# Four graph layers on one core: order of the degree, packing and normalizing steps, wider rows of pairs, and earlier loads of layer 3's mask bytes

## The chip, the cores and the metric

The kernel runs on one core of a Trainium2 chip. The metric is the device time of one launch in microseconds (us), the median of three runs. One further execution was taken with the hardware profiler; all views below are of that execution.

## What is computed

Input is x (2708 x 512, float32) and a symmetric 0/1 adjacency adj (2708 x 2708, under 1% ones). Four layers follow each other, each as `x = layernorm(x + layer(x))`:

```python
deg = max((adj != 0).sum(-1), 1)
L0: relu((dinv * (adj + I) * dinv @ x + x) @ W0 + b0)        # dinv = rsqrt(deg)
L1: (dis[:, None] * adj * dis[None, :] @ x) @ W1.T + b1      # dis = (adj.sum(1) + 1e-8) ** -0.5
L2: twice:                                                   # two attention layers
    Wh, Ws = split(x @ W2[l]); a = softmax(Wh @ Ws.T) * adj
    x = leaky_relu(a @ Wh + x, 0.01)
L3: adj @ (x @ W3) + b3                                      # 8 heads of 64 columns, as one 512-column product
```

## The kernel before, in words

**Tiles.** The 2708 nodes are 22 blocks of 128 rows; the last has 20 (block 21, "the 20-row block"). Output columns are taken in six chunks `CH` (512, 512, 512, 512, 384, 276 nodes; the last holds blocks 19, 20 and 21), input rows in six `GROUPS` (4, 4, 4, 4, 3, 3 blocks). SBUF has a pool of 82 general pages (`page`), which are used in turn, so that a new page waits for the last use of an old one; 11 wider ones (`wide`) take what the gathers fetch. PSUM has two halves of four banks (`bank`).

**Order.** Every instruction goes through `Ordered.issue` (L70 in every view), which makes each engine run its instructions in the order in which the program writes them. So the order of work is that of the Python code, engine by engine, DMA queues included: most loads and writes are issued by SP, gathers, x's writes and the residual loads (`xres`) by POOL. A blocked instruction holds all that stand behind it on its engine.

**Layers 0 and 1, and the rest of layer 3** are a list `run.seq` of steps (layer, chunk k, group g). `step` (L1066) first calls `before_products`, which loads the bytes of the adjacency (`at`) for two steps ahead (`load`) and prepares one step ahead (`prepare`, L788): ACT casts bytes to products' operands m and, in chunk 0, halves of x (`xh` on ACT, `xl` on DVE, a split of float32 in two). Then `multiply` issues PE's products into `acc`; `ends` does, a step or two later, what belongs to the chunk before: `project` (products mm with the weights), `combine` and `finish` (residual, statistics, normalizing, write). At the last group `evict` copies acc to ht. In layer 0, `examine` (L820) has DVE count and check each mask by pairs of blocks (`odd`, `part`); `degrees` (L891) adds the parts into `both` at the fifth group, and at the sixth multiplies them by ones on PE (`deg`, `cnt`), evicts these to `dg` and `cnt`, multiplies xt by dg on POOL and takes the roots (`dis`, `rdeg`). The product of the next step's acc takes the bank that deg had. The masks are written to memory as bytes and read back by all later layers. In layer 1, `prepare` also reduces the bytes by quarters of a block into `feeds` on DVE, inside the preparing.

**Packing.** After a chunk of layer 1, `index` (L1123) makes lists of the rows that each block needs, as a generator of DVE and PE stretches: products `rank` and `rest`, DVE steps keep to `up` between them, then `place`, a check of overflow (`top`, `bad`), and `one_hot` and the product `list`. `beat` (L586) runs one stretch of it at two of every three calls; `ends` and the attention's score loop call it.

**Attention.** Layers 2a and 2b run in `layer` (L1730) with a model clock (`advance`, `later`, `until`): scores sp, their greatest, shift, exponentials and sums (`soften`, L1539) on DVE and ACT; s and z (`project_steps`, L1408) are written to `pairs` in memory, a row per giver node. `fetch` (L1596) gathers 128 of these rows with one indirect DMA issued by POOL, of s and z side by side, 2,176 to 2,560 bytes of a row; `weigh` multiplies them on PE into acc. `end` and `normalize` (L1707) finish a block and write it. `pairs` is [2, rows, 768], s 128 | z 512 | s 128, so a row has a pitch of 3,072 bytes, and each z is written twice. DVE copies z out of PSUM.

**Layer 3's beginning.** During layer 2b, `early` (L599) puts the products of layer 3's first two chunks and first four groups between the attention's steps (`fill`); the sums go to pages `begun` by ACT's copies. `layer` asks for its first pieces after scores 5, 11 and 19 of the last chunk: nothing, then two loads of bytes, then `prepare` of the first four blocks (their xh and xl). Further bytes are loaded two steps ahead.

**The end.** After the last step, the run ends by `project`, `combine` and `finish` of the last chunk, block by block: 19, 20, then the 20-row block, which was computed as four partial products and is summed by a copy and three adds (`total`) and one more add.

Of the kernel before, what the change touches and what calls it, by code (L numbers as in the profile page):

```python
# [39 lines left out]
PAD = 16  # L40
FAR = 4096
# [473 lines left out]
class Fast:  # L515
# [17 lines left out]
    def run(self):  # L533
        kernel, nc = self.k, self.nc
        with ExitStack() as ctx:
# [34 lines left out]
            for i, n, ps in self.project(ly, k):  # L570
                self.finish(ly, k, [(i, n, self.combine(ly, k, 0, i, n, ps))])
# [27 lines left out]
    def early(self, run):  # L599
# [8 lines left out]
        for t in range(4 * TWO):  # L608
            ly, k, g = seq[t]
            if t < 2:  # L610
                self.attention.need(GROUPS[t + 2][1] - 1)
            self.load(*seq[t + 2])
            if t == 4:
                self.load_weights(ly)
            if t == 4 * TWO - 1:
                self.attention.need(GROUPS[4][1] - 1)
                for j in range(*GROUPS[4]):
                    ly.rows[j] = self.attention.made[j]
            self.prepare(*seq[t + 1])
            if g == 3:  # L620
                ly.begun[k] = []
            for n, j in enumerate(range(*GROUPS[g])):
                if t == 0:
                    self.multiply(ly, k, g, [j])
                else:
                    self.multiply(ly, k, g, ds=[n])
                if g == 3:
                    b = self.page(f"begun{k}_{n}")
                    self.nc.scalar.copy(b[:, : CH[k][1]], ly.acc[k][n][:, : CH[k][1]])
                    ly.begun[k].append(b)  # L630
                self.attention.advance(2 * cost(CH[k][1]))
                yield True
# [15 lines left out]
    def normalize(self, mv, rows):  # L648

# [3 lines left out]
        self.rsqrt(y, mv[:, :m, 1], LN_EPS)  # L653
# [21 lines left out]
    def rsqrt(self, dst, src, eps):  # L675
# [7 lines left out]
        nc.scalar.activation(t, v, AF.Sqrt)  # L683
        nc.vector.reciprocal(y, t)
# [63 lines left out]
    def load(self, ly, k, g):  # L748
# [6 lines left out]
        if ly.number == 0:  # L755
            tiles = []
            for j in js:
# [11 lines left out]
                for d in range(DC):  # L769
                    self.nc.sync.dma_start(at[d * QW : (d + 1) * QW, :cw], few)  # L770
        else:
            at = self.page(f"at{ly.number}_{k}_{g}", U8, (P, DC, BANK))
            self.nc.sync.dma_start(
                at[:, : len(js), :cw], self.k.masks[k][:, js[0] : js[-1] + 1, :]
            )
            tiles = [at[:, q, :] for q in range(len(js))]
            ly.done["bytes", k, g] = at
        ly.done["at", k, g] = tiles
# [9 lines left out]
    def prepare(self, ly, k, g):  # L788
# [7 lines left out]
        for j, at in zip(range(*GROUPS[g]), ats):  # L796
# [4 lines left out]
            ms.append(m)  # L801
        ly.done["m", k, g] = ms
        if ly.number == 0:
            self.examine(ly, k, g, ats)
        if ly.number == 1:
            at, (j0, j1) = ly.done.pop(("bytes", k, g)), GROUPS[g]
            feeds = self.k.feeds.rearrange("p i q j -> p j (i q)")
            i0, full = c0 // QW, cw // QW
            sets = [(j0, j1, P)] if j1 < NB else [(j0, j1 - 1, P), (j1 - 1, j1, QW)]
            for q0, q1, n in ((0, full, QW), (full, -(-cw // QW), cw % QW)):  # L810
                for a, b, rows in sets if q0 < q1 else ():
                    v = at[:rows, a - j0 : b - j0, q0 * QW : q0 * QW + (q1 - q0) * n]
                    nc.vector.tensor_reduce(
                        feeds[:rows, a:b, i0 + q0 : i0 + q1],
                        v.rearrange("p j (q i) -> p j q i", i=n),
                        AX.X,
                        ALU.max,
                    )

    def examine(self, ly, k, g, ats):  # L820
        nc, cw = self.nc, CH[k][1]
# [4 lines left out]
        for q in range(0, len(ats), 2):  # L826
# [24 lines left out]
            else:  # L851
                nc.vector.tensor_add(p, p, t)

# [37 lines left out]
    def degrees(self, ly, k, g):  # L891

        nc, cw = self.nc, CH[k][1]
        i0, n = CH[k][0] // P, len(blocks_of(k))
        if g == len(GROUPS) - 2:
            ly.both = both = self.page(f"both{k}", BF)
            if cw % P:
                nc.vector.memset(both, 0.0)
            nc.vector.tensor_add(both[:, :cw], ly.part[k][:, 0, :cw], ly.part[k][:, 1, :cw])
            return  # L900
        both = ly.both
# [3 lines left out]
        for q in range(n):  # L905
# [6 lines left out]
            )  # L912
        dg = self.page(f"dg{k}")
        nc.vector.tensor_scalar(dg[:, :cw], ps[:, :cw], 1.0, 1.0, ALU.max, ALU.add)
        cnt = self.small.tile([P, DC], FP, tag="cnt", name=f"cnt_sb{k}")[:, :n]
        nc.vector.tensor_copy(cnt, pc[:, :n])
        xt = ly.done["xt", k]
        for c in range(DC):
            nc.gpsimd.tensor_mul(xt[c][:, :cw], xt[c][:, :cw], dg[:, :cw])
        self.rsqrt(self.k.dis[:, i0 : i0 + n], cnt, DEG_EPS)  # L920
# [20 lines left out]
    def project(self, ly, k):  # L941
# [3 lines left out]
        for i, lo, n in blocks_of(k):  # L945
# [44 lines left out]
    def sum(self, ly, i, n, ps):  # L990
        nc, x = self.nc, ly.done.pop(("xres", i))
        if n <= QW:
# [15 lines left out]
    def finish(self, ly, k, parts):  # L1008
# [14 lines left out]
        return out  # L1023
# [10 lines left out]
    def before_products(self, run, t):  # L1034
# [23 lines left out]
        if t + 1 < len(seq):  # L1058
            self.prepare(*seq[t + 1])
        if ly.number == 0 and g == len(GROUPS) - 2:  # L1060
            self.degrees(ly, k, g)
# [4 lines left out]
    def step(self, run, t):  # L1066
# [19 lines left out]
        if g == (4 if ly.number == 3 and k < TWO else 3):  # L1086
            self.residual(ly, k)
            if k == len(CH) - 1 and ly is not run.layers[-1]:
                self.load_weights(run.layers[1])
        if g == len(GROUPS) - 1:  # L1090
            if ly.number == 3:
                self.biased(ly, k)
            if ly.number == 0:
                self.degrees(ly, k, g)
# [3 lines left out]
            if k in ly.acc:  # L1098
                self.evict(ly, k)
            run.before, run.phase = (ly, k), 0  # L1100
            if ly.number == 1:
# [3 lines left out]
    def ends(self, run, g):  # L1105

        nc, (ly, k) = self.nc, run.before
        if g == 0:
            run.parts = self.project(ly, k)
            run.x = []  # L1110
        if g in (0, 1):
# [11 lines left out]
    def index(self, k):  # L1123
# [80 lines left out]
        nc.vector.tensor_add(place, place, place_r)  # L1204

        top = tile_("top", [P, n], FP)
        nc.vector.tensor_mul(place_r, rank, rest[:, :, PAD:])
        nc.vector.tensor_reduce(top, place_r, AX.X, ALU.max)
        for q, (i, _, _) in enumerate(blocks_of(k)):
            room = sum(t >= nq * ONLY for ts in lists_of(i) for t in ts) * P  # L1210
            nc.vector.tensor_scalar(
                kernel.bad[:, kernel.nbad + i : kernel.nbad + i + 1],
                top[:, q : q + 1],
                1.0 - room,
                0.0,
                ALU.add,
                ALU.max,
            )
# [8 lines left out]
        for q in range(n):  # L1227
            rows, both = self.one_hot(i0 + q, row[:, q, :], which[:, q, :])
            yield "PE"
# [72 lines left out]
class Attention:  # L1302
# [7 lines left out]
    def __init__(self, fast):  # L1310
# [7 lines left out]

        self.pairs = [
            [  # L1320
                self.scratch.tile([2, NP, D + 2 * P], FP, tag=f"p{a}{b}", name=f"pairs{a}{b}")
# [9 lines left out]
    def blank(self):  # L1331

        blank = [self.page(f"blank{e}") for e in range(2)]
        for e, t in enumerate(blank):
            self.nc.gpsimd.memset(t, 0.0)
            for pairs in (p for ly in self.pairs for p in ly):
                for r in range(2):
                    c = e * D
                    w = min(D, D + 2 * P - c)
                    self.nc.sync.dma_start(pairs[r, N:, c : c + w], t[: NP - N, :w])  # L1340
# [67 lines left out]
    def project_steps(self, ly, k):  # L1408
# [19 lines left out]
        for i, lo, n in blocks_of(k):  # L1428
# [16 lines left out]
            if n > QW:  # L1445
                nc.vector.tensor_copy(z[:n], ps[:n])
            for b in range(2):
                nc.sync.dma_start(
                    ly.pairs[b][:, i * P : i * P + n, P : P + D].rearrange("r j d -> j r d"),
                    z[:n].unsqueeze(1).to_broadcast([n, 2, D]),  # L1450
# [79 lines left out]
    def load_masks(self, ch):  # L1530
        for j0, j1 in GROUPS:
            a = self.page(f"a{ch.name}_{j0}", U8, (P, DC, BANK))
            self.nc.sync.dma_start(
                a[:, : j1 - j0, : ch.cw], self.k.masks[ch.k][:, j0:j1, :]
            )
# [3 lines left out]
    def soften(self, ch):  # L1539
# [23 lines left out]
        for q0, q1, w in self.parts(ch):  # L1563
            for side in range(2):
                qs = [q for q in range(q0, q1) if q % 2 == side]
                if not qs:
                    continue
                r0, m, c = qs[0] // 2, len(qs), side * (P + D)
                e = ch.s[j][:n, qs[0] * P : qs[0] * P + w].unsqueeze(1)
                if m > 1:  # L1570
                    e = ch.s[j][:n, :].rearrange("j (r x) -> j r x", x=2 * P)
                    e = e[:, r0 : r0 + m, side * P : side * P + w]
                nc.sync.dma_start(
                    ch.ly.pairs[ch.k % 2][
                        r0 : r0 + m, j * P : j * P + n, c : c + w
                    ].rearrange("r j i -> j r i"),
                    e,
                )
# [17 lines left out]
    def fetch(self, ch):  # L1596
# [5 lines left out]
        if q not in ch.x:  # L1602
# [7 lines left out]
        h = t // ONLY if t < QUARTERS * ONLY else (0, QUARTERS - 1)[q % 2]  # L1610
        first, width = (P, D + (h + 1) * QW) if q % 2 else (h * QW, D + P - h * QW)
# [3 lines left out]
            in_=ch.ly.pairs[ch.k % 2].rearrange("r j d -> (r j) d"),  # L1615
            in_offset=bass.IndirectOffsetOnAxis(ap=self.k.givers[:, i, t : t + 1], axis=0),
            element_offset=(q // 2) * NP * (D + 2 * P) + first,
# [25 lines left out]
    def weigh(self, wait=False):  # L1643
# [18 lines left out]
        for h, g in enumerate(gs):  # L1662
            lo, m = (0, w) if len(gs) == 1 else (h * QW, QW)
            e, z = (D + lo, 0) if q % 2 else (0, P - lo)
# [42 lines left out]
    def normalize(self, ch):  # L1707
        self.f.normalize(ch.mv, [(r, r, w) for r, w in ch.ends])
        for (i, _, _), (r, _) in zip(ch.blocks, ch.ends):
            self.nc.sync.dma_start(self.k.saved[2][i], r)  # L1710
            self.made[i] = r
# [18 lines left out]
    def layer(self, ly, chunks, fill):  # L1730
        f = self.f
        self.chunks, self.made = chunks, {}
        for k, ch in enumerate(chunks):
# [4 lines left out]
            for n, j in enumerate(js):  # L1738
# [15 lines left out]
                if n in (5, 11, 19) and k + 1 == len(chunks):  # L1754
# [17 lines left out]
        self.shift_rows(last)  # L1772
        self.until(self.clock + 3, fill)
# [112 lines left out]
```

## Time and profile before

| | |
|---|---|
| runs | 2347.88, 2351.14, 2351.31 us (median 2351.14) |
| profiled execution | 2336.56 us, of which the span is 2334.30 |
| busy of PE | 2275.3 us, 97% |
| busy of DVE, ACT, POOL | 1428.0, 663.8, 708.3 us |
| mean granted clock of PE | 0.99 |
| DMA | 463.50 MB, 199 GB/s over the span |

A line of the page's groups gives line, engine, operation, output and inputs, count, then busy time and mean ns of one, then the idle time ahead of them on that engine and what ended it. In a timeline a row gives start, duration, and in brackets the idle time before and its releaser. Busy times of DVE, ACT and POOL lie under PE's wherever PE doesn't wait for them. The page's slices show the kernel's stages: layer 0's groups end at 303 us, layer 1 reduces its bytes into feeds until 606, scores of the attention run from 780 to 1971, the products of what was gathered from 945 to 2117 in two stretches (POOL's two high stretches), and layer 3's last products start at 2318:

```profile
DVE  6777886786655529658667511228769778624523
POOL 3334431111000000635466450001635557452000
```

### The profile page before, as it was taken

The page shows a single profiled execution, that of the slowest core. Times are in us where ns is not written, and L with a number is a line of the kernel's source. Part 1 is how long each engine was busy: PE and PEld are TensorE (multiplying, and loading weights), DVE is VectorE, ACT ScalarE, POOL GpSimd, SP SyncE. Part 2 cuts the span into 40 slices and gives each one's busy share as a digit, 9 for nine tenths or more (in the row PEclk, how much of TensorE's full clock was granted, in tenths as well). Part 3 has the DMA queues.
Part 4 walks back from the last instruction along what each step waited for, and adds up shares of the span by engine and source line. Part 5 has one row for each costly group of instructions (what it writes and reads, how often), then busy time and mean ns, then how long its engine had stood idle before and what let it go on. Part 6 is the DMA issues. An engine that isn't in the chain of part 4 may idle for free. (4 is left out here: it accounts for less than half of the span.)

```text
span 2334.3 us, 26143 instructions
## 1 busy us (share of the span) xinstructions
PE 2275.3 (97%) x8525; PEld 1293.5 (55%) x8525; DVE 1428.0 (61%) x2832; ACT 663.8 (28%) x1334; POOL 708.3 (30%) x823
## 2 busy tenths in 40 slices
PE   9999999999999999999999999999999999899997
PEld 6676767778644444443555444444443455565675
DVE  6777886786655529658667511228769778624523
ACT  7444352222110123223232210113222324431211
POOL 3334431111000000635466450001635557452000
PEclk9999999999999999999999999999999999899999
DMA  9966652222434404869699996305868799883311
GB/s 339 292 179 174 177 176 79 75 81 79 174 132 175 146 0 148 304 211 307 217 342 327 299 381 245 136 5 165 297 220 292 251 308 333 282 270 116 116 50 43
DMA packets 324247, 463.50 MB, mean 199 GB/s; under 512 B 66370, under 2 KB 201962, under 8 KB 324100
## 3 DMA queue, kind: packets, MB, share of 16 engines
q1 hardware_dynamic: 255444, 246.57, 32.1%
q0 software_dynamic: 68656, 215.15, 27.7%
q8 instruction: 69, 1.13, 0.2%
q14 instruction: 78, 0.64, 0.1%
HBM read 307.75 MB, written 153.85 MB: 198 GB/s over the span
## 5 line engine op out<-in xcount | busy, mean ns | idle before, releaser
L70 PE MATMUL sp<-xs,wst_sb 128*128 128x512 f32 (+3 forms) x2112 | 800.2, 545 | 0.0
L70 POOL DMA_INDIRECT g<-pairs,givers x510 | 526.5, 1032 | 881.0 <-issue 372.8
L70 PEld LDWEIGHTS sp<-xs,wst_sb 128*128 128x128 f32 (+1 forms) x2112 | 380.2, 186 | 409.8 <-issue 326.2
L70 PE MATMUL acc<-m,xh 128*128 128x512 f32 (+4 forms) x1584 | 569.8, 381 | 17.8 <-ACT begun L70 8.3
L70 PE MATMUL acc<-m,xl 128*128 128x512 f32 (+4 forms) x1584 | 552.4, 367 | 0.5 <-DVE xl L70 0.5
L70 PEld LDWEIGHTS acc<-m,xh 128*128 128x128 f32 (+1 forms) x1584 | 290.3, 189 | 84.0 <-issue 23.6
L70 PEld LDWEIGHTS acc<-m,xl 128*128 128x128 f32 (+1 forms) x1584 | 290.5, 190 | 45.5 <-issue 5.3
L70 PE MATMUL acc<-g 128*32 128x512 f32 (+1 forms) x1020 | 261.4, 609 | 2.5 <-DMA g<-pairs,givers 2.3
L70 ACT ACTIVATE s<-s 128x512 f32<-128x512 f32 (+3 forms) x264 | 151.5, 579 | 334.6 <-DVE s L70 334.5
L70 ACT COPY s<-sp 128x512 f32<-128x512 f32 (+2 forms) x252 | 132.6, 528 | 400.2 <-PE sp L70 397.2
L70 DVE TENSOR_TENSOR top<-top,s 128x512 f32<-128x512 f32 (+2 forms) x240 | 149.2, 622 | 152.1 <-ACT s L70 149.7
L70 PE MATMUL mm<-w,ht 128*128 128x512 f32 (+1 forms) x528 | 224.2, 596 | 5.0 <-DVE ht L70 5.0
L70 ACT CAST m<-at 128x512 fp32r<-128x512 uint8 (+5 forms) x396 | 199.3, 566 | 75.3 <-DMA at<-mask 38.0
L70 DVE TENSOR_TENSOR s<-s,shift 128x512 f32<-128x512 f32 (+3 forms) x264 | 162.6, 619 | 34.2 <-ACT shift L70 34.2
L70 DVE TENSOR_TENSOR s<-s,a 128x512 f32<-128x512 f32 (+3 forms) x264 | 166.1, 629 | 20.3 <-DMA a<-mask 11.3
L70 DVE TENSOR_TENSOR sum<-sum,s 128x512 f32<-128x512 f32 (+4 forms) x252 | 156.5, 621 | 17.4 <-ACT s L70 17.4
L70 PEld LDWEIGHTS mm<-w,ht 128*128 128x128 f32 (+1 forms) x528 | 96.2, 187 | 122.1 <-issue 111.3
L70 PE MATMUL wst<-xt,mixed 128*128 128x512 f32 (+2 forms) x384 | 151.0, 545 | 1.9 <-ACT mixed L70 1.9
L70 PEld LDWEIGHTS acc<-g 128*32 128x32 f32 (+1 forms) x1020 | 74.6, 135 | 140.5 <-issue 116.6
L70 PE MATMUL z<-w,xt 128*128 128x512 f32 (+1 forms) x352 | 151.0, 596 | 0.0
L70 DVE COPY z_sb<-z 128x512 f32<-128x512 f32 (+1 forms) x44 | 30.3, 690 | 178.3 <-PE z L70 175.1
L70 POOL DMA_DIRECT2D x<-o x44 | 26.0, 597 | 357.0 <-DVE o L70 352.8
(168 smaller groups left out, 1543.6 us busy)
## 6 DMA issues: line engine op xcount, KB each, us to landing
pairs<-s SPq DMA_DIRECT2D x378, 128.0 KB
pairs<-z_sb SPq DMA_DIRECT2D x84, 512.0 KB
at<-in_adj_t SPq DMA_DIRECT2D x84, 256.0 KB
xres<-x POOLq DMA_DIRECT2D x44, 256.0 KB
x<-o POOLq DMA_DIRECT2D x43, 256.0 KB
x<-x SPq DMA_DIRECT2D x37, 256.0 KB
at<-mask SPq DMA_DIRECT2D x32, 256.0 KB
xt<-t SPq DMA_DIRECT2D x32, 256.0 KB
```

The source lines that it names most:

```text
L70: ins = call(*args, **kw)
```

## The change

It touches the order of several stages and the shape of one memory tensor.

1. `examine` of layer 0 becomes a generator that stops after each pair of blocks. For chunks above 0, in group 0, only the first pair is examined at `prepare`; the rest (`checked`) follows the eviction of the chunk before.
2. `degrees` is split: `degree_ends` makes the products, then dg and cnt, then the multiplications and roots. At the last chunk of layer 0 its middle part runs after the first cast of the next step's `prepare`, whose reduction into feeds (`note`) and layer 1's weight loads come after the eviction. `before_products` no longer prepares across the layer boundary.
3. In `index` the check (top, bad) runs behind the first `one_hot`; one more `beat` comes in `ends` at the last chunk of layer 1.
4. z of layer 2a is evicted by ACT, no longer by DVE.
5. `pairs` has one row of 2,048 floats per node, z 512 | s 256 | z 512 | s 256 | z 512; z is written three times, s in pieces of 256 floats; gathers take their parts from these rows. The pages for mask bytes are as wide as the chunk, not 512, so that the pieces of a load join.
6. The normalizing in layer 2b stops after the root's issue on ACT; the rest is put 4 us of the model clock later.
7. `layer` asks for layer 3's halves no longer after score 19 but after `shift_rows`; `early` loads bytes five groups further ahead (`load_bytes`).
8. At the end of layer 3 the 20-row block is projected first, is summed by four adds straight into x, and is normalized together with block 19; block 20 follows.

```diff
             ly, k = run.before
-            for i, n, ps in self.project(ly, k):
-                self.finish(ly, k, [(i, n, self.combine(ly, k, 0, i, n, ps))])
+            parts = self.project(ly, k)
+            for some in (parts[:-1], parts[-1:]):
+                made = []
+                for i, n, ps in some:
+                    made.append((i, n, self.combine(ly, k, len(made), i, n, ps)))
+                self.finish(ly, k, made)
...
             ly, k, g = seq[t]
+            for later in seq[t + 2 if t == 0 else t + 6 : t + 7]:
+                self.load_bytes(*later)
             if t < 2:
                 self.attention.need(GROUPS[t + 2][1] - 1)
...
         nc.scalar.activation(t, v, AF.Sqrt)
+        yield True
         nc.vector.reciprocal(y, t)
...
+    def load_bytes(self, ly, k, g):
+        if ("bytes", k, g) in ly.loaded:
+            return
+        ly.loaded.add(("bytes", k, g))
+        (j0, j1), cw = GROUPS[g], CH[k][1]
+        at = self.page(f"at{ly.number}_{k}_{g}", U8, (P, DC, cw))
+        self.nc.sync.dma_start(at[:, : j1 - j0, :], self.k.masks[k][:, j0:j1, :])
...
         if ly.number == 0:
-            self.examine(ly, k, g, ats)
+            self.examining = self.examine(ly, k, g, ats)
+            if k == 0 or g > 0:
+                self.checked()
+            else:
+                next(self.examining)
...
-        for i, lo, n in blocks_of(k):
+        for i, lo, n in sorted(blocks_of(k), key=lambda b: b[2] > QW):
...
         nc, x = self.nc, ly.done.pop(("xres", i))
+        if n <= QW and ly.number == 3:
+            for c in range(DC):
+                nc.vector.tensor_add(x[:n], x[:n], ps[c * QW : c * QW + n, :])
+            return x
...
-        if t + 1 < len(seq):
+        if t + 1 < len(seq) and seq[t + 1][0].number == ly.number:
             self.prepare(*seq[t + 1])
...
-            if k == len(CH) - 1 and ly is not run.layers[-1]:
-                self.load_weights(run.layers[1])
...
             if ly.number == 0:
-                self.degrees(ly, k, g)
+                ends = self.degree_ends(ly, k)
+                next(ends)
+                if k == len(CH) - 1:
+                    note = self.prepare(
+                        *run.seq[t + 1], between=lambda: next(ends), late=True
+                    )
+                for _ in ends:
+                    pass
...
                 self.evict(ly, k)
+            if ly.number == 0:
+                self.checked()
             run.before, run.phase = (ly, k), 0
+            if ly.number == 0 and k == len(CH) - 1:
+                note()
+                self.load_weights(run.layers[1])
...
+            if ly.number == 1 and k == len(CH) - 1:
+                self.beat()
...
             rows, both = self.one_hot(i0 + q, row[:, q, :], which[:, q, :])
+            if q == 0:
+                examine()
             yield "PE"
...
-                self.scratch.tile([2, NP, D + 2 * P], FP, tag=f"p{a}{b}", name=f"pairs{a}{b}")
+                self.scratch.tile([NP, 2 * PAIR + D], FP, tag=f"p{a}{b}", name=f"pairs{a}{b}")
...
-            if n > QW:
+            if n > QW and a == 0:
+                nc.scalar.copy(z[:n], ps[:n])
+            elif n > QW:
                 nc.vector.tensor_copy(z[:n], ps[:n])
             for b in range(2):
+                rows = ly.pairs[b][i * P : i * P + n, :]
                 nc.sync.dma_start(
-                    ly.pairs[b][:, i * P : i * P + n, P : P + D].rearrange("r j d -> j r d"),
-                    z[:n].unsqueeze(1).to_broadcast([n, 2, D]),
+                    bass.AP(rows.tensor, rows.offset, [rows.ap[0], (PAIR, 3), (1, D)]),
+                    z[:n].unsqueeze(1).to_broadcast([n, 3, D]),
                 )
...
     def normalize(self, ch):
-        self.f.normalize(ch.mv, [(r, r, w) for r, w in ch.ends])
-        for (i, _, _), (r, _) in zip(ch.blocks, ch.ends):
-            self.nc.sync.dma_start(self.k.saved[2][i], r)
-            self.made[i] = r
+        work = self.f.normalizing(ch.mv, [(r, r, w) for r, w in ch.ends])
+        next(work)
+        def rest():
+            for _ in work:
+                pass
+            for (i, _, _), (r, _) in zip(ch.blocks, ch.ends):
+                self.nc.sync.dma_start(self.k.saved[2][i], r)
+                self.made[i] = r
+        self.later(4, rest)
...
-                if n in (5, 11, 19) and k + 1 == len(chunks):
+                if k + 1 == len(chunks) and n in ((5, 11, 19) if ly.number == 0 else (5, 11)):
                     next(fill)
...
         self.shift_rows(last)
+        if ly.number == 1:
+            next(fill)
         self.until(self.clock + 3, fill)
```

## The prediction

> **What bounds the kernel now.** I read the page's busy times, then PE's waits, then the timelines of the engines at each of those waits, and the chain for the end.
>
> ```profile
> PE 2275.3 (97%) x8525; PEld 1293.5 (55%) x8525; DVE 1428.0 (61%) x2832; ACT 663.8 (28%) x1334; POOL 708.3 (30%) x823
> ```
>
> PE is the bound: 97% of the 2334.3 us span. No product is removed, so only PE's idle time, its slow time and the end can go. The waits of PE ("waited for: us in total, times, longest us"):
>
> ```profile
> PE acc L70 <- ACT begun L70: 8.3, 1, 8.3
> PE acc L70 <- DVE dg L70: 6.3, 2, 5.3
> PE mm L70 <- DVE ht L70: 5.0, 3, 2.3
> PE list L70 <- DVE both L70: 4.2, 3, 2.7
> PE rest L70 <- DVE up L70: 3.5, 1, 3.5
> PE tr_mx L70 <- DVE wide L70: 3.5, 1, 3.5
> PE acc L70 <- ACT m L70: 3.2, 1, 3.2
> PE tr_top L70 <- DVE top L70: 2.7, 1, 2.7
> PE acc L70 <- DMA g<-pairs,givers: 2.3, 5, 0.6
> ```
>
> With the smaller ones about 42 us in all, nearly every line a single event. Some are paid twice. Two stretches of the windows (start and end, length, busy time of PE, PEld, DVE, ACT and POOL, granted clock, DMA share, GB/s):
>
> ```profile
> 658.00:668.00 10.00, 6.46 (x17) 2.65 (x17) 9.00 (x31) 1.17 (x2) 1.51 (x3) 1.00 0.15 57
> 2026.30:2036.50 10.20, 5.70 (x13) 4.46 (x14) 5.21 (x14) 7.28 (x16) 1.00 (x1) 0.50 0.75 202
> ```
>
> After the 8.30 us gap the clock is 0.50 for 10.2 us, and a product takes 0.80 us rather than 0.39. Such stretches follow the gaps at 66.8, 303.7, 408.5, 782.8, 1981.4, 2022.1 and 2130.9 (3.4, 6.8, 3.4, 3.4, 3.4, 10.2 and 3.4 us): 34 us at half rate, 17 lost. The 3.54 us gap at 658.7 and the 2.67 us one at 1912.3 brought none. With the 19.5 us tail (2314.8 to 2334.3), some 78 us are to be had at most; each part below gets its share.
>
> **The change part by part** (gain in us, then both ends).
>
> *First examine deferred.* Ahead of dg (62.48) DVE runs odd, odd and an add of part, 0.69 each; they go behind evict: 2.06 us earlier dg and ht, against gaps of 0.98 (dg) and 2.25 (ht), and 1.7 of half clock. In the later chunks DVE stood idle before dg, so nothing changes there. 3.0 (2.0 to 3.7).
>
> *Degrees at the layer boundary.* PE's 5.35 us wait at 303.7 is the product that needs the bank which dg empties. On DVE (start, duration, what it is):
>
> ```profile
> 306.79 2.29 DVE L70 TENSOR_REDUCE feeds<-at 128x64 bf16<-128x2048 uint8 x1
> 308.98 0.43 DVE L70 TENSOR_SCALAR dg<-deg 128x276 f32<-128x276 f32 x1
> ```
>
> dg (0.43) moves ahead of the later xl's, which waited 4.67 and 0.90 us, and of the 2.29 us reduce: deg's product ends near 303, so dg is there by some 304, and load_weights' five DMAs on POOL go behind the xt multiplications. Late next is ht: the xl's (to 306.9) and the dis steps still stand ahead of it. mm moves from 317.5 to some 312. 5.5 (4.5, nearly the gap, to 8.8, with the half clock).
>
> *The list's check moved.* top and four bad's (404.21 to 404.83, 0.6) leave the chain to both at 408.5, a 1.24 us gap whose half clock costs 1.7. 2.0 (0.5 to 2.2).
>
> *z evicted on ACT, one more beat.* keep to up (658.33 to 662.76, 4.4 us) stood behind the three combines (641 to 658); now they come right behind rank at 640. At 782.8 the next chain stood behind a z copy that waited for PE until 778.80; that copy (0.69 on DVE, about 0.59 on ACT) leaves DVE. Waits 3.54, 0.31, 0.56, 2.68 and 1.7 half clock: 8.8. ACT is busy 13.6 of 100 us there. 8.0 (3.5 to 8.8).
>
> *Root apart, first halves put off.* At 1907.24 DVE waits 3.61 us for a root (ACT: a copy and a table load of 1.28), then runs five small steps and four r's ahead of top; PE waits 2.67. Now top goes between. At 1981.4 PE waits 3.45 for wide and 1.7 follow: the xl's of layer 3 leave that stretch, one 1.84 us product step comes between tr_top and tr_mx, but the first xl then is ready only at about 1976.5 for products that now start at 1973.7, a new wait of some 2.5. Together 4.2 (-1 to 7.8).
>
> *Bytes five groups ahead.*
>
> ```profile
> 2023.05 0.49 SPq L70 DMA_DIRECT2D at<-mask  x1
> 2028.09 2.18 ACT L70 CAST m<-at 128x512 fp32r<-128x512 uint8 x4 [7.32 <-DMA at<-mask]
> 2030.17 0.57 ACT L70 COPY begun<-acc 128x512 f32<-128x512 f32 x1
> 2030.80 0.80 PE L70 MATMUL acc<-m,xh 128*128 128x512 f32 x1 [8.30 <-ACT begun L70]
> 2130.80 0.62 ACT L70 CAST m<-at 128x512 fp32r<-128x512 uint8 x1 [6.57 <-DMA at<-mask]
> ```
>
> SP issues the bytes in order behind pairs<-s (at 2023.05), the casts wait 7.32 us for them, and PE for the copy behind the casts: 8.30 + 5.1 half clock = 13.4. At 2130.9 it is the same, behind x<-r: 3.21 + 1.7 = 4.9. With bytes there, ACT's work at 2125 is done by 2127.8, before PE needs it at 2131.3. 17.9 (8 to 18.3: the begun copy alone, half clock kept; all). Queued behind the new DMAs on SP: pairs<-s and x<-x, which the gathers and residuals need. Five pages of 82 are held longer.
>
> *The tail.* Three rounds in a row on DVE; of the chain of what ended last:
>
> ```profile
> 2324.76 0.69 DVE xres L70
> ...
> 2327.78 0.53 DVE o L70
> ```
>
> The 20-row block is last: a copy, four adds, then 3.0 us of normalizing, to 2328.31. First instead of last, its four adds, st and mv (3.7 us from about 2312) lie under the other blocks' products; those two normalize together, and block 20's products end near 2319.1, its own round (xres 0.7, st 0.7, rest 2.2, by the rows of 2318.4 to 2322.0) near 2323.5. 4.8 less 0.6 for a last write of 128 rows rather than 20: 4.2 (3 to 5).
>
> *DMA pieces.* s goes out in pieces of 1 KB instead of 512 B, z three times instead of two (84 DMAs of 512 KB become 768: +21.5 MB of 463.5), and a gathered row comes from one pitch of 8 KB instead of 3 KB; gather bytes are the same. The stretch where z goes out:
>
> ```profile
> 1290.00:1410.00 120.00, 117.65 (x362) 48.69 (x360) 40.13 (x88) 19.91 (x43) 57.75 (x61) 1.00 0.96 343
> 1410.00:1500.00 90.00, 90.00 (x250) 43.16 (x250) 16.73 (x25) 9.62 (x20) 0.00 (x0) 1.00 0.57 205
> ```
>
> Some 6 MB more before 1410 at 377 GB/s is 16 us of queue, taken up behind 1410, where 0.43 of 90 us is free. PE waits 2.3 for gathers now. Value 0; from +2.3 to a loss: each percent on a packet costs 1.2 + 0.8 us in 1290 to 1410 and in 1926 to 2008, both near share 1.0. x's reads from an 8 KB pitch (xs<-t) take a median 84 ns per 2 KB packet, as contiguous ones do, so I take no loss. A rule against the change: the Trainium skill, "DMA: Bandwidth & Descriptors", section "🔬 Latency and other measured facts", has copies at a row pitch of large powers of two slowed (512 KiB 207 GB/s, 4 MiB 103) and advises padding. Its smallest pitch is 64 times this one; if it held here at its worst, the gathers would double and the change lose, and the row of xs<-t speaks against that.
>
> Sum: 3.0 + 5.5 + 2.0 + 8.0 + 4.2 + 17.9 + 4.2 + 0 = 44.8; the ends are 20 and 57. Against it, an earlier PE meets gathers that POOL issues every 1.26 us in 1926 to 2008, and a half-clock stretch can come behind another gap, as 1.24 us brought one and 3.54 none: I take three such (5 us). 40 us: the profiled execution (2336.56, its span and 2.3 around it) becomes 2296.6. It ran 14.6 below the median of the runs, 2351.1, so that becomes 2311.
>
> **Rivals.** *(a) Small gain.* New waits (gathers, the first xl, half-clock stretches by phase) take back more than half: only 5 to 20 us are left, 2331 to 2346. For it: POOL's pitch, and DMA share 1.00 in 1926 to 2008. Against: the largest terms are waits on one late load each. *(b) The bytes don't come early.* The loads ahead sit in SP's order behind x<-x, which waits for pages (17.5 us in 16 waits on x<-x): begun stays late, 17.9 go, 2329; counted with (a). *(c) Slower.* The 8 KB pitch slows gather packets. At 25% DMA needs 120 x (0.96 x 1.25 - 1) = 24 us more in 1290 to 1410 and 82 x 0.25 = 20.5 more in 1926 to 2008, where gathers already set the pace: 44.5, all of the gain. From there it decides; at 40% it is 41 + 33 = 74, 2381. For it: z's extra bytes fall where DMA is full. Against: xs<-t.
>
> **How the numbers follow.** Forecast (gain 20 to 57, 2294 to 2331): 0.68. (a) with (b), 5 to 20: 0.17. No change within 0.2% (4.7 us, about what a measurement of this kernel can tell): 0.05. (c): 0.10. Faster is 0.85. The range leaves out (c) and the outermost of the forecast: 2296 to 2342.
>
> **What would show it.** Right: PE's list of waits lacks begun, dg at the boundary, up and m; ACT has no at<-mask wait over 2 us after 1975; PEclk has no stretch at 2020 to 2040; the chain at the end has no mm_sb. Wrong: PE waits for g of over 10 us, a packet of the gather clearly longer, or at<-mask still behind pairs<-s.

## The result, and the profile after

| | median | runs | ratio to the kernel before |
|---|---|---|---|
| before | 2349.6 us | 20, 2345.5 to 2357.5 | |
| changed | 2332.7 us | 20, 2325.4 to 2349.5 | 0.9933 (0.9919 to 0.9948) |

By the ratio 15.7 us are gained (12.2 to 19.0), where 40 were forecast. The time lies inside the predicted range, but in the piece that belonged to rival (a), 5 to 20 us. One thing has to be known to read the numbers below: on one of the chips that the experiments ran on the kernel before took 2334 to 2336 us, on three others 2344 to 2348, so every version is given as a ratio to the kernel before on the same chip. The profile that the prediction was made from (2336.6) looks like those of the quicker chip, and the changed kernel's below (2333.96, span 2332.2) like those of the others; the last section says by what.

The page's busy times and PE's list of waits in the changed kernel:

```profile
PE 2281.0 (98%) x8525; PEld 1291.3 (55%) x8525; DVE 1408.7 (60%) x2803; ACT 675.3 (29%) x1354; POOL 705.9 (30%) x822
PE acc L71 <- issue: 14.4, 13, 9.9
PE acc L71 <- ACT m L71: 5.9, 4, 3.1
PE mm L71 <- DVE ht L71: 4.0, 3, 1.4
PE acc L71 <- DMA g<-pairs,givers: 3.5, 4, 1.4
PE acc L71 <- ACT begun L71: 1.7, 1, 1.7
```

dg, up, top and wide are gone, begun is down from 8.3 to 1.7. New are 9.9 us with no releaser in the profile, and more waits for m. By the starts of the same products in both profiles, the changed kernel is 10.5 us ahead behind the layer boundary (312.96 to 302.47), 11.8 at the first scores (779.7 to 767.9), 10.7 at the last scores (1971.0 to 1960.3), and then 5.2 *behind* at the last product of gathered rows (2117.7 to 2122.9). That one stage took 146.7 us and takes 162.6. There DVE shows this, first in the kernel before, then in the changed one (start, duration, instruction, idle time before it and its releaser):

```profile
1995.42 0.38 DVE L70 TENSOR_SCALAR rs_v<-mv 128x4 f32<-128x4 f32 x1
1996.06 0.18 DVE L70 RECIPROCAL rs_y<-rs_t 128x4 f32<-128x4 f32 x1 [0.27 <-ACT rs_t L70]
...
2040.91 0.75 DVE L70 SCALAR_TENSOR_TENSOR xr<-acc,rden,xr 128x512 f32<-128x512 f32 x1
```

```profile
1993.91 0.17 DVE L71 TENSOR_SCALAR rs_v<-mv 128x4 f32<-128x4 f32 x1
2009.88 0.75 DVE L71 SCALAR_TENSOR_TENSOR xr<-acc,rden,xr 128x512 f32<-128x512 f32 x1 [15.80 <-remote]
...
2012.95 0.14 DVE L71 RECIPROCAL rs_y<-rs_t 128x4 f32<-128x4 f32 x1
```

The fourth chunk's normalizing begins at 1993.91 and goes on at 2012.95. Between stands xr of the fifth chunk's first block, which needs the sum of rows still being gathered; in the kernel before this xr comes 45 us behind the normalizing. What brings it forward can be read in the code (it was not tried apart): layer 3's beginning calls `need` for the fourth chunk's blocks, and until these are in `made`, which the put-off rest does, `need` issues products of gathered rows. These run the model clock on, and the fifth chunk's xr comes due before the rest. ACT shows what waits behind them (the first cast's page is released by the r that follows xr, the second by a write of r to memory):

```profile
2011.39 0.62 ACT L71 CAST m<-at 128x512 fp32r<-128x512 uint8 x1 [14.47 <-DVE r L71]
2018.95 0.62 ACT L71 CAST m<-at 128x512 fp32r<-128x512 uint8 x1 [6.20 <-DMA x<-r]
```

PE then starves in small pieces from 2010 to 2032 (0.8, 0.9, 1.0, 1.4, 3.1), with 10.2 us of half clock. The other loss of this stage is the wait for the first xl, which the put-off halves have behind another xr:

```profile
1970.26 0.75 DVE L71 SCALAR_TENSOR_TENSOR xr<-acc,rden,xr 128x512 f32<-128x512 f32 x1 [8.60 <-issue]
1974.41 0.79 PE L71 MATMUL acc<-m,xl 128*128 128x512 f32 x1 [9.92 <-issue]
```

The tail is as foreseen, one round fewer. Its last o ends at 2324.62, 13.1 us after the last group of products mm began; before it was 17.1 us.

```profile
2313.23 2.83 DVE L71 TENSOR_TENSOR xres<-xres,mm 20x512 f32<-20x512 f32 x4 [1.11 <-PE mm L71]
2324.07 0.55 DVE L71 TENSOR_SCALAR o<-xres,mv,y 128x512 f32<-128x512 f32 x1
```

### The profile page after: what moved, and what is told of

Same layout as the page of the kernel before. It is cut to its first block, busy times and chain, and to the rows that moved or that the text cites. A ratio compares the mean times of both kernels' runs of the same rounds, so it can differ in the third digit from the quotient of the medians.

```text
span 2332.2 us, 25904 instructions
## 1 busy us (share of the span) xinstructions
PE 2281.0 (98%) x8525; PEld 1291.3 (55%) x8525; DVE 1408.7 (60%) x2803; ACT 675.3 (29%) x1354; POOL 705.9 (30%) x822
## 4 chain that ended last, share of the span: by engine, by line
PE 83%; DVE 6%; DMA 4%; issue 3%; POOL 1%; ACT 1%; another core or an unknown queue 1%; SPq 0%; POOLq 0%; DVEq 0%; ACTq 0%
PE sp L71 30%; PE acc L71 29%; PE mm L71 8%; PE z L71 6%; PE wst L71 6%; DMA g<-pairs,givers 1%; POOL g L71 1%; DVE s L71 1%; DMA at<-in_adj_t 1%; DMA x<-in_x 1%; DVE sum L71 1%; PE mix L71 1%; PE list L71 1%; PE tr_x2b L71 1%
## 5 line engine op out<-in xcount | busy, mean ns | idle before, releaser
L71 PE MATMUL acc<-g 128*32 128x512 f32 (+1 forms) x1020 | 268.2, 606 | 6.9 <-DMA g<-pairs,givers 3.5
L71 DVE TENSOR_TENSOR sum<-sum,s 128x512 f32<-128x512 f32 (+4 forms) x252 | 156.9, 623 | 15.9 <-ACT s L71 13.6
L71 DVE SCALAR_TENSOR_TENSOR xr<-acc,rden,xr 128x512 f32<-128x512 f32 (+1 forms) x44 | 32.8, 747 | 140.0 <-PE acc L71 77.5
```

The lines of the kernel that those rows point to most:

```text
L71: ins = call(*args, **kw)
```

## Theories and experiments

**A**: the loss sits where layer 2b passes into layer 3, in the order given to DVE, ACT and SP. **B**: the wider rows of pairs and z's third write load the DMA engines everywhere.

### One part undone

*Root together again:*

```diff
-        work = self.f.normalizing(ch.mv, [(r, r, w) for r, w in ch.ends])
-        next(work)
...
-        self.later(4, rest)
+        self.f.normalize(ch.mv, [(r, r, w) for r, w in ch.ends])
...
```

> The changed kernel with one part undone: layer 2b normalizes at once again, no longer 4 us of the model clock after the root. Theory A (what is lost is lost where layer 2b passes into layer 3, by the order that DVE, ACT and PE are given there): the rest of the normalizing stands behind xr of the next chunk, which waits 15.8 us at 2009.9, and holds back the r's, xl's and m's; that wait goes, and with it PE's gaps of 0.8 + 1.0 + 1.0 + 1.4 + 3.1 + 0.3 = 7.5 and half-clock stretches worth 5 between 2010 and 2036; tr_top's wait of 2.7 near 1905 comes back: 8 to 10 us faster than the changed kernel, about 2323. Theory B (wider rows of pairs and the third write of z load the DMA engines, so gathers and loads are late everywhere): within 3 us of the changed kernel, 2333, with the waits for g and for xr still there.

0.9890 (0.9875 to 0.9905): 10 us better than the changed kernel, as A has it. The stage takes 144.3 us.

*Halves after score 19 again:*

```diff
-                if k + 1 == len(chunks) and n in ((5, 11, 19) if ly.number == 0 else (5, 11)):
+                if k + 1 == len(chunks) and n in (5, 11, 19):
...
-        if ly.number == 1:
-            next(fill)
```

> The changed kernel with layer 3's first halves prepared after score 19 again. Theory A: PE's wait of 9.9 us for the first xl near 1964 and the 10.2 us of half clock behind it (5.1) go, the wait for wide (3.5, and 1.7 of clock) comes back: about 10 us faster than the changed kernel, 2323. Theory B: the xl's are late because xr is late by DMA, which no order changes: within 3 us, 2333.

0.9917 (0.9900 to 0.9934): not to be told from 0.9933 (one execution of the six, at 4736.8 us, is left out). The 9.9 us wait went, but one at tr_mx (5.1) and one for m (7.9) stood in its place, and the half clock of this stage stayed at 20.5 us.

*Bytes two groups ahead only:*

```diff
-            for later in seq[t + 2 if t == 0 else t + 6 : t + 7]:
-                self.load_bytes(*later)
```

> The changed kernel with layer 3's bytes loaded two groups ahead only, as before. By the prediction, which gave the bytes 17.9 us, it is 13 to 18 us slower than the changed kernel, 2346 to 2351, with a wait of ACT for at<-mask of over 5 us ahead of the begun copies. If theory A holds and the root and the halves have made the casts late for other reasons, the bytes are worth less than 8: under 2341.

0.9936 (0.9921 to 0.9950): in the changed kernel the bytes ahead are worth nothing that can be told. The wait for begun is 2.1, not over 5.

*Old tensor of pairs* (shape [2, rows, 768], z twice, s in 512-byte pieces, the gathers' offsets as before):

```diff
-                self.scratch.tile([NP, 2 * PAIR + D], FP, tag=f"p{a}{b}", name=f"pairs{a}{b}")
+                self.scratch.tile([2, NP, D + 2 * P], FP, tag=f"p{a}{b}", name=f"pairs{a}{b}")
```

> The changed kernel with the old tensor of pairs: two planes with rows of 768 floats, z written twice, s in pieces of 512 bytes, gathers from those rows. Theory A: within 3 us of the changed kernel, 2333, the waits at 1964 and 2010 still there. Theory B: the new waits between 1077 and 1300 (1.4, 1.0, 2.0, 0.9) and the late xr go: 10 to 15 us faster, about 2320.

0.9907 (0.9890 to 0.9924), between the theories. But the new stalls near 1210 and 1274 are still there, and the products of layer 2b's gathers begin at 1635.2, later than the changed kernel's 1631.5: what B explains by the rows is there without them. That 0.9907 lies below 0.9933 is not explained by this; the intervals touch.

### The kernel before again, and parts alone

> The kernel before, unchanged, for a second profile. If the profiled execution that the prediction was made from (2336.6, below all of the timed runs of the kernel before) was a typical one, this profile has the same waits of PE in the same places, within 3 us at the end of each stage. If it was a lucky one, the stage between the last scores of layer 2b and the last product of gathered rows is 8 to 13 us longer here than the 146.7 us there.

Span 2348.3. The stage takes 151.2, 4.5 us more than in the prediction's profile, not 8 to 13. The rest of the 14 us is spread: 6 by the first gathers' products of layer 2b, 3.7 more by the last scores. The 15.9 us by which that stage grew are then 11.4 against a profile of the same kind: by it the changed kernel is 20.4 us ahead at the last scores and 9.0 at the last product of gathered rows.

*Root apart in the first three chunks only:*

```diff
-        self.later(4, rest)
+        if ch.k < 3:
+            self.later(4, rest)
+        else:
+            rest()
```

> The changed kernel with the root apart for the first three chunks of layer 2b alone, and normalizing at once from the fourth on. Theory A, now that normalizing at once everywhere brought some 10 us against the changed kernel: only the fourth chunk's rest stands behind an xr that waits for gathers, so the 10 us are kept and the wait for top near 1905 (2.5 and a half-clock stretch of 6.8, 3.4) goes too: about 0.9880 of the kernel before, 2 to 5 us better than with all of it undone. If the root apart costs in every chunk: as the changed kernel, 0.993.

0.9878 (0.9855 to 0.9900). The fourth chunk alone carried the cost; that 0.9878 is better than 0.9890 is not shown. Its normalizing now runs through, and the stage takes 147.6 us:

```profile
1986.06 0.17 DVE L71 TENSOR_SCALAR rs_v<-mv 128x4 f32<-128x4 f32 x1
1986.50 0.18 DVE L71 RECIPROCAL rs_y<-rs_t 128x4 f32<-128x4 f32 x1 [0.27 <-ACT rs_t L71]
```

*Root apart alone, on the kernel before* (the diff's `normalizing`, the `yield` in `rsqrt` and `later(4, rest)`, nothing else):

> The kernel before with this alone: layer 2b's normalizing stops after the root, its rest 4 us of the model clock later. Theory A: the rest of the fourth chunk stands behind the next chunk's first xr, so r's, xl's and m's of layer 3 come late also here; 5 to 12 us slower than the kernel before. If the loss needs the other parts (halves put off, bytes ahead): within 3 us of it, or 2.7 faster by top.

1.0039 (1.0023 to 1.0055), 9 us slower, with the same picture and a stage of 162.3 us:

```profile
2007.69 0.17 DVE L70 TENSOR_SCALAR rs_v<-mv 128x4 f32<-128x4 f32 x1
2022.97 0.75 DVE L70 SCALAR_TENSOR_TENSOR xr<-acc,rden,xr 128x512 f32<-128x512 f32 x1 [15.11 <-remote]
2026.04 0.15 DVE L70 RECIPROCAL rs_y<-rs_t 128x4 f32<-128x4 f32 x1
```

*Front alone* (the changed kernel with root, halves, bytes, pairs and tail undone):

> The changed kernel with the root, the halves, the bytes, the rows of pairs and the tail undone: what is left are the edits of layers 0 and 1, of the packing and of the projection. The prediction gave these 3.0 + 5.5 + 2.0 + 8.0 = 18.5 us; the profile of the changed kernel shows 16.7 by 800 us. If what is gained there lasts to the end: 16 us faster than the kernel before, 0.993. If an earlier PE meets gathers that keep their pace in layer 2a (the changed kernel is only 11 ahead by 1300): 9 to 12 us, 0.9955.

0.9931 (0.9912 to 0.9950), 16 us: as much as the whole change. What an earlier PE lost to gathers in layer 2a is not visible in the end.

### With the root together, one more part undone

These four ran on the quicker chip, where the kernel before took 2335.7. The root together with nothing else undone was not measured there; the changed kernel was, at 0.9892 (below).

> The changed kernel with the root apart and the bytes ahead both undone. The kernel with the root alone undone ran at 0.9890 of the kernel before. Theory A': the bytes were worth nothing in the changed kernel because the casts were late behind the root's rest anyway; with that gone, their gain shows: 8 to 13 us, so 0.9925 to 0.9945, with a wait for begun of over 4 us and one for m at the 32-row product of over 3. Rival: the bytes' gain is small in any company (casts wait for pages or for ACT's own queue): 0.9885 to 0.991.

0.9876 (0.9859 to 0.9893): as the rival says, or better.

> The changed kernel with the root apart and the putting off of the first halves both undone (prepared after score 19 again). The putting off was forecast at 1 to 2 us of gain; the profile with the root alone undone still shows PE waiting 6.6 us for the first xl, and 10.2 us of half clock. If that wait is its price: 5 to 9 us faster than 0.9890, that is 0.985 to 0.987. If the wait for wide and for top that it had removed (3.5 and 1.7 of clock in the profile of before) comes back in its place: 0.988 to 0.990.

0.9896 (0.9881 to 0.9912).

> The changed kernel with the root apart undone and the old tensor of pairs. With the rows of 2,048 floats undone alone the changed kernel ran at 0.9907, by 0.9933. Theory B in part: z's third write and the long rows cost 5 to 8 us in any company: 0.986 to 0.9875. If that difference came only with the late rest, or is chance: 0.988 to 0.990.

0.9885 (0.9868 to 0.9903): no cost of the rows is shown. B falls as the main cause; a few us stay possible.

> The changed kernel with the root apart and the new order of the last blocks both undone. By the prediction the tail is worth 4.2 us; the profile of the changed kernel has 20.7 us from the last group of products mm to the end, that of before 23.0, so 2.4. Expected 2 to 4 us slower than 0.9890: 0.990 to 0.9907, and 23 us from the last 24 products mm to the end in the profile.

0.9902 (0.9888 to 0.9917). From the last group of products mm to the end 23.1 us, against 20.5 to 20.8 in the three others: the tail is worth some 2.5.

### Where the bytes' gain went

*Bytes ahead alone, on the kernel before* (`load_bytes` and the loop in `early`):

> The kernel before with the bytes loaded five groups ahead alone. By the prediction's step 8 to 18 us faster than the kernel before, 0.992 to 0.9965, without the waits for begun and for m. If these waits are replaced by others (pages held longer, xl's behind xr): within 4 us, 0.998 to 1.002.

0.9971 (0.9960 to 0.9981), 6.8 us. PE no longer waits for begun, and not at the 32-row product, but at nearly the old place for m:

```profile
1995.72 0.63 ACT L70 ACTIVATE xh<-x 128x512 fp32r<-128x512 f32 x1 [7.95 <-DMA x<-x]
2007.55 0.62 ACT L70 CAST m<-at 128x512 fp32r<-128x512 uint8 x1 [5.59 <-DMA x<-r]
2008.22 0.80 PE L70 MATMUL acc<-m,xh 128*128 128x512 f32 x1 [5.78 <-ACT m L70]
```

and SP's order suggests why: five loads of bytes first, then the loads of x, then the writes of r, which hold pages until 2007:

```profile
1980.49 3.40 SPq L70 DMA_DIRECT2D at<-mask  x5
1984.76 4.12 SPq L70 DMA_DIRECT2D x<-x  x4
...
1997.58 6.06 SPq L70 DMA_DIRECT2D x<-r  x4
```

*Root, bytes and halves all undone:*

> The changed kernel with the root apart, the bytes ahead and the halves put off all undone. If bytes and halves cover each other (each undone without the root: 0.9876 and 0.9896, against 0.9890): 0.9905 to 0.993, with a wait for begun of over 4 us. If neither is worth anything: 0.9875 to 0.9895.

0.9904 (0.9891 to 0.9917). The wait for begun is back:

```profile
PE acc L71 <- ACT begun L71: 5.4, 1, 5.4
```

Against it the halves put off alone (0.9876) gain some 6 us, with intervals that just touch, the bytes alone (0.9896) 2, not told from nothing: with the halves put off and no bytes ahead the wait for begun is 2.1, so what I gave to the bytes goes mostly with the halves.

*Root apart in three chunks, bytes not ahead:*

> The version that the results point to: the changed kernel with the root apart in the first three chunks of layer 2b alone and the bytes loaded two groups ahead. If the gain of the one (0.9878 against 0.9890) and of the other (0.9876) are real and add: 0.9865, the fastest. If they are chance: 0.9875 to 0.989.

0.9860 (0.9844 to 0.9876), 2300.3 us: the fastest measured, 33 us under the kernel before. Only small waits of PE are left:

```profile
PE acc L71 <- ACT m L71: 4.4, 2, 3.3
PE acc L71 <- DVE xl L71: 3.2, 2, 1.7
PE mm L71 <- DVE ht L71: 2.7, 2, 1.4
```

*The changed kernel on the same chip:*

> The changed kernel itself, on the chip of the other three, and a second profile of it. If its profile was a typical one: 0.992 to 0.995, xr of the fifth chunk waiting over 10 us ahead of the fourth's rs_y, and 160 us or more between the last scores and the last product of gathered rows. If that profile was an odd one, the wait is below 5 us and the stage near 150.

0.9892 (0.9877 to 0.9908), 25 us gained, below the 0.992 to 0.995 that I expected. xr still stands ahead of rs_y, but waits 10.3 us, and the stage takes 147.7. Against the prediction's profile it is 21.9 us ahead at the last scores and 20.9 at the last product of gathered rows: here the stage loses 1 us, not 11. And the four versions above with the root together (0.9876 to 0.9902) are not clearly quicker than this, so that the root apart costs anything on this chip is not shown by the times.

*Bytes ahead, behind x and r on SP; and the root together once more:*

```diff
             self.prepare(*seq[t + 1])
+            for later in seq[5 if t == 2 else t + 6 : t + 7] if t > 1 else ():
+                self.load_bytes(*later)
```

> The version of some_bytes with the bytes loaded ahead again, but from the third step of layer 3 on, behind that step's loads of x and cast, and so on SP behind the loads of x and the writes of r that the first two steps need. If the bytes' gain was lost to what stood behind them on SP: the waits of some_bytes for m at the 32-row product (3.3, and 3.4 of clock) and for begun (1.0) go and no wait of ACT for x<-r or x<-x over 4 us comes in 1980 to 2010: 3 to 6 us faster than some_bytes, 0.9835 to 0.985 in runs where the kernel before takes 2334. If loading ahead holds pages that others wait for whenever it is done: 0.986 to 0.988.

> The changed kernel with the root apart undone, a second time. Where the kernel before takes 2344 to 2350, as in its first run, 0.989 again. Where it takes 2334 and the changed kernel has 0.9892: theory A with its size: DVE waits 10.3 us there for the gathers instead of 15.8, PE lost about 5 less, so 0.986 to 0.988; if the root apart costs nothing there: 0.9885 to 0.990.

The kernel before took 2345.1 beside these: 0.9869 (0.9853 to 0.9886) and 0.9909 (0.9893 to 0.9926). No wait for x<-r is left in the first, and the waits at the 32-row product and for begun are gone, but against 0.9878 for the same kernel with the bytes as changed the intervals overlap: that their place on SP decides is argued from alone_bytes' rows, not shown by the time. The second puts the root's gain at 6 us against 10 in its first run, with an interval that overlaps the changed kernel's.

## Why the prediction was wrong, step by step

- **Root apart** is the step that failed. It said "Now top goes between" and looked at the place near 1907 alone, where that is so. The same code runs for the fourth chunk at 1995, where before's DVE went on after 0.27 us, and there xr goes between, which waits 15.8 us: `need` asks for the blocks whose rest was put off and pulls the fifth chunk ahead of it. The model clock's 4 us took 19 on the chip (1993.91 to 2012.95). With the halves the step was given +4.2 with an end at -1; the root alone costs 9 us (5.4 to 12.9), and undone it gave 10, and 6 the second time, not told from nothing. All three were measured where the kernel before takes 2344 us or more.
- **Bytes ahead**, 17.9, mis-sized: 6.8 alone, nothing that shows in company. The 8.3 us wait was not the bytes' alone: 5.8 for m took its place, with the half clock kept (10.2 us of it, as before). Only the second wait, 3.2 and its clock 1.7, went wholly; these are most of the 6.8.
- **First halves put off**: its new wait was foreseen ("ready only at about 1976.5", 2.5 us) and came as 9.9 in the changed kernel's profile, behind an xr that waited 8.6; in the other versions that keep it as 1.6 to 2.1 on the quicker chip and 1.7 to 9.0 on the others. What it gave, some 6 us by begun, was not foreseen.
- **Front** (first examine, degrees, check, z on ACT), 18.5 forecast: right, 16 measured alone. At the layer boundary mm begins at 307.1 instead of 317.5, where I had 312 (the same products, of block 19, at 309.7: the new order of blocks holds in all layers); what was late next was m and xl at 331 (1.1 and 1.5), and the lead falls from 10.5 to 6.5 us there.
- **Tail**, 4.2: 2.5. The round saved is there (17.1 to 13.1 us, 4.0, where I had 4.8); the last write and what follows cost 7.6 instead of 6.0, where I had 0.6 more.
- **DMA pieces**, 0: no run shows them to differ from that, though undoing them read 6 us better once, 0.9907 by 0.9933. PE waits 3.5 us for g, not over 10, and the packets of gathered rows take a median 196 ns in both kernels' profiles (1620 to 1920), so rival (c) is out. The Trainium skill's row on row pitch ("DMA: Bandwidth & Descriptors", section "🔬 Latency and other measured facts") begins at 512 KiB. At the 8 KB here no run shows a slowing.
- **The base**: the profile was of the quicker kind, the median not. On the quicker chip the change gains 25 us, in the runs of the result 16. Between the two profiles of the kernel before, 14.0 us apart, 6 arise by layer 2b's first gathered rows and 8 behind them; the prediction carried its offset of 14.6 over unchanged, through the stages that it changed.

None of the prediction's signs of being wrong pointed at the failed step: g, the packets and at<-mask behind pairs<-s are as they should be. The list of PE's waits was added up to about 42 us, it is 44; nothing rests on that.

The added parts (16 + 6.8 + 2.5 - 9) give 16, near what is measured, but they were measured on different chips and don't simply add: bytes and halves take away one wait between them.

## What to carry to other kernels

A step that is put later in an in-order queue must be followed at every place where the code runs, not at the one where the profile shows the wait: what matters is which waiting instruction then stands ahead of it, and who asks meanwhile for what the step makes. The price of a wait is what remains when the next releaser comes, so of a late load on a shared queue the next loads and page writes are to be timed as well. And a base profile is to be held against the runs first: here it lay below all of them.

## What the runs showed that I had not expected

The same kernel takes 2334 us on one chip (measured twice) and 2344 to 2348 on three others. The kept traces show two things that go with it. All eight profiles from the quicker chip, and the one that the prediction was made from, have no wait of PE without a releaser; all ten from the others, and the changed kernel's first, have 7 to 15 us of such waits. And where DVE's xr waits over 3 us for a sum (1950 to 2035), it starts 0.04 to 0.15 us after the last product's end in the one group, 0.9 to 6.0 in the other. In the changed kernel's first profile that product is this, which xr follows at 2009.88:

```profile
2004.60 1.12 PE L71 MATMUL acc<-g 128*128 128x512 f32 x2 [0.34 <-issue]
```

So 4.2 of the 15.8 us are not the gathers' time, and with them goes most of the difference to the 10.3 on the quicker chip. What happens in these 4.2 us the profile does not tell, and why one chip differs stays open.
